# A graph attention kernel in two layers: paired statistics, the tiles of one row sum chain, and when the values are scaled

## The chip, the cores and the metric

The kernel runs on one core of one Trainium2 chip. The metric is the device time in microseconds of one execution, the median of several runs. In the profile the engines are named PE (TensorE, matmuls), PEld (its weight loads), DVE (VectorE), ACT (ScalarE), POOL (GpSimd) and SP (SyncE, which issues most of the transfers).

## The reference

Two graph attention layers follow one another on x of shape 8 x 2048 x 256 (batches, rows, channels) with one adjacency matrix of 2048 x 2048. After each layer its input is added and every row is normalised.

```python
# layer 0: 8 heads of 32 channels
x_proj = einsum('bnd,hdf->bhnf', x, W)
e = leaky_relu(e_src[..., :, None] + e_dst[..., None, :], 0.2)
e = e + softplus(beta_tilde) * log(adj + 1e-6)      # and no edge where adj is 0
h = softmax(e) @ x_proj
x1 = layernorm(x + h.reshape(B, N, D) @ W_out.T)
# layer 1: one head, dot products
e = leaky_relu((x1 @ W1) @ (x1 @ W2).T, 0.2)        # and no edge where adj is 0
out = layernorm(x1 + relu(softmax(e) @ (x1 @ W3)))
```

## The kernel before, in words

**Layer 0** (class `Gat`, one object a batch) never forms the softmax as such. The score of an edge is a function of a sum of two numbers, so its exponential is a maximum of two products. For a unit, which is one pair of heads (`hp`, 4 of them) and one tile of 128 source rows (`jt`, 16 of them), VectorE makes for each of the two heads a tile `s` of 128 x 2048 by one instruction at L375, out of the query rows `c`, a factor `re` and the adjacency tile `mt`. TensorE multiplies `s` by the scaled values `v` into `val` and, for the row sum of the softmax, by the broadcast factor `re` into `den` (both in `products`, L403 to L408). There are 4 buffers for `s`, so VectorE can be two units ahead of TensorE, and 2 buffers for `mt`, which is loaded again from memory for every unit (L202).

**The row sum chain** takes some of the den products away from TensorE. The table `SUMMED` (L68, L69) lists for each batch and pair the tiles that are chained. For the first of them ScalarE makes `d`, a copy of `s` scaled by the factor (L392). For each later one VectorE adds the scaled `s` to `d`, one unit later (L386). For these tiles there is no den product; after the last tile one product with ones adds `d` to `den` (L397). Each later chain tile costs VectorE two long instructions, and saves TensorE one den product.

**Layer 1** (class `Dot`) takes 16 steps a batch: scores, exponential, transposes and the product with h3, with row statistics at the end. Its matmuls are full size, and its work for VectorE is small.

**The order.** TensorE's order is written out by hand; the other engines' instructions are put in order by the framework, by program order and by when they are ready in its own model. The main loop (L668 on) puts the layer 0 of batch b, called `fresh`, between the steps of the layer 1 of batch b - 1 through `layer_0(n)`, which runs n units. Batch 0 has no partner; its 64 units come first and share their time with `others()` (L603), which projects all other batches. Every second unit is followed by a slot in which some rows of it are projected (L658 to L662).

The first pair of each fresh batch has a place of its own: its 16 units lie around the end of the batch before. Units 0 to 5 share it with two steps of the old layer 1. Then six groups follow, with two units in each of the first five: groups 0 to 3 make x1 (`output`, four row tiles at a time: matmul with W_out, addition of x, statistics, normalisation), groups 2 to 5 turn it (`turn`: transposes and h3). Before the first group VectorE also has to multiply the heads by the reciprocal row sums (`finish`, L448). Tile numbers in what follows are these units.

**x1's statistics** (L476 to L483): for each row tile of 256 channels one `bn_stats`, which writes count, mean and sum of squared deviations for the even and for the odd elements, and one `bn_aggr`, which joins them to mean and variance.

**The scaling of the values** (`scale`, L290 to L294) multiplies the projected values of a quarter of a batch by the factor, 128 x 1024 elements. `factors()` (L276) has to precede it, and `store()` (L296) follows for the batches whose values go to memory. `others()` holds a list `later` with the three scalings and the store that remain, and takes one entry off at every row it projects (L635).

Of the kernel before, what the change touches and what calls it, by code (L numbers as in the profile page):

```python
# [9 lines left out]
F32 = mybir.dt.float32  # L10
BF16 = mybir.dt.bfloat16
I32 = mybir.dt.int32
AF = mybir.ActivationFunctionType
ALU = mybir.AluOpType
# [4 lines left out]
P = 128  # L19
# [8 lines left out]
def kernel(  # L28
# [26 lines left out]
    nc = tc.nc  # L55
    B, N, D = x.shape
    H, _, DH = w_proj.shape
# [3 lines left out]
    NB = N // BK  # L61
    HALF = N // 2
    HP = 2
    NP = H // HP
    IG = BK // P


    SUMMED = [[()] * NP, [()] + [(1, 4, 7, 10, 13)] * (NP - 1)]  # L68
    SUMMED += [[(2, 4, 5)] + [(1, 3, 5, 7, 9, 11, 13)] * (NP - 1)] * (B - 2)  # L69

    const = ctx.enter_context(tc.tile_pool(name="const", bufs=1))
    dram = ctx.enter_context(tc.tile_pool(name="dram", bufs=1, space=DRAM))
# [3 lines left out]
    small = ctx.enter_context(tc.tile_pool(name="small", bufs=3))  # L76
# [3 lines left out]
    def mm_tile(name):  # L80
        return ps.tile([P, BK], F32, tag="mm", name=name)
# [15 lines left out]
    eps_ln = const.tile([P, 1], F32)  # L97
# [36 lines left out]
    def later_weights():  # L134

        nc.sync.dma_start(w3s, w3.rearrange("(k p) d -> p k d", p=P))
        w1t, w2t = (chunk.tile([P, KC, D], F32, tag="pt", name=name, bufs=2) for name in ("w1t", "w2t"))
        for w, dst in ((w_out, wot), (w1, w1t), (w2, w2t)):
            src = [row_tile("square") for _ in range(KC)]
            for o in range(KC):  # L140
                nc.sync.dma_start(src[o], w[ts(o, P), :])
            yield
            for kc in range(KC):
                t = mm_tile("sq_t")
                for o in range(KC):
                    nc.tensor.transpose(t[:, ts(o, P)], src[o][:, ts(kc, P)], ident)
                nc.scalar.copy(dst[:, kc, :], t[:, 0:D])
        yield
        for dc in range(KC):
            t = mm_tile("w12p")  # L150
            for kc in range(KC):
                nc.tensor.matmul(t[:, 0:D], w1t[:, kc, ts(dc, P)], w2t[:, kc, :], start=(kc == 0), stop=(kc == KC - 1))
            nc.scalar.copy(w12[:, dc, :], t[:, 0:D])
        yield
# [75 lines left out]
    def row_tile(name, bufs=4):  # L230
        return small.tile([P, D], F32, tag="row", name=name, bufs=bufs)


    class Gat:
# [216 lines left out]
        def output(self):  # L451


            b = self.b
            xb = x[b].rearrange("(t p) d -> p t d", p=P)
            xs = []

            def load(g):
                xs.append(chunk.tile([P, IG, D], F32, tag="ht", name="xg", bufs=3))
                nc.sync.dma_start(xs[g], xb[:, ts(g, IG), :])  # L460

            load(0)
            yield
            for g in range(NB):
                if g < NB - 1:
                    load(g + 1)
                st = small.tile([P, IG, nc.vector.BN_STATS_DIM], F32, name="st4", bufs=1)
                mv = small.tile([P, IG, nc.vector.BN_AGGR_DIM], F32, name="mv4", bufs=2)
                z = self.ht[:, ts(g, IG)].rearrange("p t k i -> p t (k i)")
                for k in range(0, IG, 2):  # L470
                    y = mm_tile("y").rearrange("p (t c) -> p t c", t=2)
                    for i in range(2):
                        for kc in range(KC):
                            nc.tensor.matmul(y[:, i, :], self.ht[:, g * IG + k + i, kc, :], wot[:, kc, :],  # L474
                                             start=(kc == 0), stop=(kc == KC - 1))
                    nc.vector.tensor_add(z[:, k:k + 2, :], y, xs[g][:, k:k + 2, :])  # L476
                    for i in range(k, k + 2):
                        nc.vector.bn_stats(st[:, i, :], z[:, i, :])
                        nc.vector.bn_aggr(mv[:, i, :], st[:, i, :])
                f = small.tile([P, 2, IG], F32, name="f4", bufs=2)  # L480
                nc.scalar.activation(f[:, 0, :], mv[:, :, 1], AF.Ln, bias=eps_ln)
                nc.scalar.activation(f[:, 0, :], f[:, 0, :], AF.Exp, scale=-0.5)
                nc.vector.scalar_tensor_tensor(f[:, 1, :], mv[:, :, 0], -1.0, f[:, 0, :], ALU.mult, ALU.mult)  # L483
                for k in range(IG):
                    nc.scalar.activation(z[:, k, :], z[:, k, :], AF.Identity, bias=f[:, 1, k:k + 1],
                                         scale=f[:, 0, k:k + 1])
                nc.scalar.dma_start(x1_d[b].rearrange("(t p) d -> p t d", p=P)[:, ts(g, IG), :], z)
                yield
# [114 lines left out]
    def others():  # L603


        order = gats[2:-2] + gats[1:2] + gats[-2:]
        groups = [(gat, g) for gat in order for g in range(NB)]
        xgs, xts, later = [], [], []

        def load(n):  # L610
            if n < len(groups):
                xgs.append(load_x(groups[n][0].b, groups[n][1]))

        def turn(n):
            if n < len(groups):
                xts.append(chunk.tile([P, KC, BK], F32, tag="ht", name="xt", bufs=3))
                transpose_x(xgs[n], xts[n])
                load(n + 1)

        load(0)  # L620
        yield
        turn(0)
        for n, (gat, g) in enumerate(groups):
            if g == 0:
                if gat is order[-1]:

                    for _ in range(IG):
                        later.pop(0)()
                        yield
                gat.begin("h3" if n // NB % 2 or gat is order[-1] else "v")  # L630
            for k in range(IG):
                gat.row(g * IG + k, xts[n])
                if k == 1:
                    turn(n + 1)
                if later:  # L635
                    later.pop(0)()
                if g == NB - 1 and k == IG - 1:
                    gat.factors()
                    gat.scale(0)
                    later = [lambda gat=gat, i=i: gat.scale(i) for i in range(1, NB)]  # L640
                    if gat.b > 1:
                        later.append(gat.store)
                if g == 0 and k == IG - 1 and n > 0:
                    groups[n - 1][0].queries()
                yield
        for work in later:
            work()
        order[-1].queries()
        yield

    projections, weights = others(), later_weights()
    next(projections)
    count = (B - 1) * NT + IG
    for k in range(1, NP * NT + 1):
        g0.step()
        if k == NP * NT:
            gats[1].load_ahead()
        if k % 2 == 0:  # L658
            for _ in range(k * count // (NP * NT) - (k - 2) * count // (NP * NT)):
                next(projections)  # L660
            if k > NT:
                next(weights, None)  # L662

# [4 lines left out]
    for b in range(1, B + 1):  # L668
        gat, fresh = gats[b - 1], gats[b] if b < B else None

        def layer_0(count):
            if fresh:
                fresh.step(count)

        if b > 1 and fresh:
            fresh.follow(gat)
            values = fresh.load()
            next(values)
            fresh.later.append(values)
        rows, turns = gat.output(), gat.turn()  # L680
        if dot is None:
            layer_0(4)
            next(projections)
            next(rows)
        else:

            dot.step(lambda k: layer_0((0, 2, 2)[k]))
            if not fresh:
                for work in gat.later:
                    for _ in work:  # L690
                        pass
            next(rows)
            dot.step()
        layer_0(2)

        for g in range(NB + 2):
            if g < NB:
                next(rows)
            if g > 1:
                next(turns)  # L700
                if g == NB + 1:
                    dot = Dot(gat)
                next(turns)
            if g < NB + 1:
                layer_0(2)
        dot.scores(0)
        dot.step(lambda k: layer_0((2, 0, 2)[k]))
        count = NP * NT - 20
        for i in range(NT - 3):
            n = (i + 1) * count // (NT - 3) - i * count // (NT - 3)  # L710
            dot.step(lambda k: layer_0((0, n - 2, 2)[k]))
# [31 lines left out]
```

## Time and profile before

| what | value |
|---|---|
| time, median of 3 runs | 4389.91 us (4386.79 to 4391.33) |
| span of the profiled execution | 4393.1 us |
| mean granted TensorE clock | 0.989 |
| `s`, L375 | 1024 instructions, 2342 ns each |
| chain additions, L386 | 264 instructions, 2344 ns each |
| chain copies, L392 (ScalarE) | 54 instructions, 2006 ns each |
| x1's bn_stats, L478, and bn_aggr, L479 | 128 of each, 411 and 169 ns |
| scaling, L294 | 32 instructions, 1219 ns each |
| VectorE waiting for `mt` transfers | 58.3 us in 33 waits |

The line numbers are those of the kernel before. The busy time of TensorE is a union of its instructions, and a matmul's end is modelled, so that a stretch with TensorE busy throughout needn't be one at full rate; the granted clock stands beside it for that. A line of a timeline gives start, length, engine, line, operation and tiles, how many instructions are merged in it, and in brackets the idle time before it with what ended it. In a list of waits, a line gives who waited for whom, the total, the number of waits and the longest.

### The profile page before, as it was taken

The numbers are of one execution on the slowest core, as the hardware profiler recorded it, in microseconds if no ns is written. First come the engines' busy times: TensorE is split into PE (matmuls) and PEld (weight loads), VectorE is DVE, ScalarE is ACT, GpSimd is POOL, SyncE is SP. The second block draws the span as 40 slices with busy tenths as digits, with TensorE's granted clock in tenths as the row PEclk, the third lists the DMA queues.
The fourth block names the chain that finished last, engine by engine and source line by source line (L and its number), as shares of the span: only waits on it lengthen the run. The fifth ranks groups of instructions, "written<-read, shape, count | busy, mean of one in ns | idle before, by whom it ended". The sixth has DMA issues, their size and how long they took to land.

```text
span 4393.1 us, 59809 instructions
## 1 busy us (share of the span) xinstructions
PE 4245.8 (97%) x25072; PEld 2220.1 (51%) x25072; DVE 3603.9 (82%) x2606; ACT 1661.8 (38%) x3019; POOL 9.5 (0%) x14
## 2 busy tenths in 40 slices
PE   7999899998999999999999999999999999999999
PEld 4444354544555545554555545555455545555666
DVE  6888878988799989889789988989799987998222
ACT  6522143332433333333343333333333324333455
POOL 0000000000000000000000000000000000000000
PEclk9999999999999999999999999999999999999999
DMA  8877756656455564556555464555544565543211
GB/s 251 303 256 262 264 193 221 223 191 229 174 192 190 204 213 148 194 183 217 193 180 199 159 232 171 195 187 211 194 177 167 183 224 191 184 174 143 78 48 41
DMA packets 253166, 839.10 MB, mean 191 GB/s; under 512 B 32224, under 2 KB 150752, under 8 KB 178400
## 3 DMA queue, kind: packets, MB, share of 16 engines
q1 hardware_dynamic: 217568, 801.71, 51.5%
q10 hardware_dynamic: 35328, 33.56, 2.3%
q8 instruction: 196, 3.21, 0.3%
q14 instruction: 74, 0.61, 0.0%
HBM read 761.53 MB, written 73.14 MB: 190 GB/s over the span
## 4 chain that ended last, share of the span: by engine, by line
PE 56%; DVE 20%; issue 8%; DMA 7%; ACT 2%; SPq 1%; POOL 0%; DVEq 0%; ACTq 0%; POOLq 0%
DVE s L375 14%; PE e L534 14%; PE val L406 12%; PE acc L573 12%; PE den L406 9%; PE pt L557 3%; DMA mt<-mt_d 3%; DVE d L386 3%; PE h3p L505 2%; PE h1p L524 2%; DMA rb<-rec_d 1%; DVE p L539 1%; DMA xg<-in_x_dram 1%; PE y L474 1%; PE proj L270 1%
## 5 line engine op out<-in xcount | busy, mean ns | idle before, releaser
L375 DVE SCALAR_TENSOR_TENSOR s<-c,re,mt 128x2048 f32<-128x2048 f32 x1024 | 2353.6, 2342 | 225.4 <-PE den L406 150.8
L406 PE MATMUL val<-s,v 128*32 128x512 f32 x8192 | 1041.2, 606 | 84.9 <-DVE s L375 84.9
L573 PE MATMUL acc<-h,pts 128*128 128x256 f32 x4096 | 954.4, 381 | 16.7 <-ACT pts L559 16.6
L534 PE MATMUL e<-x1t,h 128*128 128x512 f32 x2048 | 904.5, 594 | 3.3 <-ACT h L526 3.2
L573 PEld LDWEIGHTS acc<-h,pts 128*128 128x128 f32 x4096 | 747.9, 190 | 113.0 <-ACT pts L559 28.4
L406 PE MATMUL den<-s,re 128*32 128x512 f32 x5648 | 727.1, 601 | 0.0
L386 DVE SCALAR_TENSOR_TENSOR d<-s,re,d 128x2048 f32<-128x2048 f32 x264 | 615.0, 2344 | 0.0
L534 PEld LDWEIGHTS e<-x1t,h 128*128 128x128 f32 x2048 | 380.2, 190 | 450.1 <-issue 415.6
L406 PEld LDWEIGHTS val<-s,v 128*32 128x32 f32 x8192 | 245.6, 110 | 707.1 <-issue 517.1
L559 ACT COPY pts<-pt 128x512 f32<-128x512 f32 x512 | 296.3, 582 | 690.2 <-PE pt L557 689.4
L539 DVE CUSTOM_DVE_ANT_0 p<-p,pen 128x2048 f32<-128x2048 f32 x128 | 292.6, 2286 | 225.3 <-ACT p L536 225.1
L536 ACT ACTIVATE p<-e 128x512 f32<-128x512 f32 x512 | 304.4, 595 | 455.4 <-PE e L534 447.7
L406 PEld LDWEIGHTS den<-s,re 128*32 128x32 f32 x5648 | 198.0, 112 | 436.1 <-issue 429.7
L557 PEld LDWEIGHTS pt<-ident,p 128*128 128x128 f32 x2048 | 239.0, 141 | 219.8 <-issue 174.7
L542 ACT ACTIVATE p<-p,neg 128x2048 f32<-128x2048 f32 x128 | 256.7, 2005 | 208.5 <-DVE neg L539 208.5
L557 PE MATMUL pt<-ident,p 128*128 128x128 f32 x2048 | 318.1, 279 | 5.1 <-ACT p L542 5.1
L579 DVE TENSOR_TENSOR z<-z,x1r 128x256 f32<-128x256 f32 x128 | 54.0, 422 | 182.9 <-ACT z L578 181.5
L578 ACT ACTIVATE z<-acc,rec 128x256 f32<-128x256 f32 x128 | 60.6, 473 | 373.4 <-PE acc L573 286.8
L270 PE MATMUL proj<-wp,xt 128*128 128x272 f32 (+1 forms) x512 | 130.9, 401 | 2.3 <-ACT v L272 1.2
L505 PE MATMUL h3p<-w3s,x1t 128*128 128x256 f32 x512 | 122.7, 383 | 4.8 <-ACT x1t L500 4.3
L272 ACT COPY v<-proj 128x256 f32<-128x256 f32 x128 | 46.9, 376 | 206.4 <-PE proj L270 192.4
L474 PE MATMUL y<-wot,ht 128*128 128x256 f32 x512 | 118.3, 385 | 0.0
(89 smaller groups left out, 1926.8 us busy)
## 6 DMA issues: line engine op xcount, KB each, us to landing
mt<-mt_d SPq DMA_DIRECT2D x496, 1024.0 KB
c<-c_d SPq DMA_DIRECT2D x64, 1024.0 KB
pen<-pen_d SPq DMA_DIRECT2D x112, 512.0 KB
xg<-in_x_dram SPq DMA_DIRECT2D x60, 512.0 KB
adj_t<-in_adj_dram SPq DMA_DIRECT2D x16, 1024.0 KB
mt_d<-mt SPq DMA_DIRECT2D x16, 1024.0 KB
rb<-rec_d SPq DMA_DIRECT2D x128, 128.0 KB
x_d<-ht ACTq DMA_DIRECT2D x32, 512.0 KB
```

Source lines behind the costliest of these rows:

```text
L270: nc.tensor.matmul(t[:, 0:cols], xt[:, kc, ts(it % IG, P)], wp[:, kc, 0:cols], start=(kc == 0), stop=(kc == KC - 1))
L375: nc.vector.scalar_tensor_tensor(sa, self.cs[a], self.re[:, 0, jt, h:h + 1], mt, ALU.max, ALU.mult)
L386: nc.vector.scalar_tensor_tensor(d, sa, e[:, jt - 1, h:h + 1], d, ALU.mult, ALU.add)
L406: nc.tensor.matmul(dst[ts(q, DH), ts(c, BK)], weights[q % 2], s[q % 2][:, ds(q // 2 * HALF + c * BK, BK)], start=start, stop=stop)
L505: nc.tensor.matmul(t[:, ts(i, D)], x1t[:, kc, ts(2 * (j - 1) + i, P)], w3s[:, kc, :], start=(kc == 0), stop=(kc == KC - 1))
L534: nc.tensor.matmul(t, self.h1[:, kc, ts(it % IG, P)], self.x1t[:, kc, ts(c, BK)], start=(kc == 0), stop=(kc == KC - 1))
L536: nc.scalar.activation(p[:, ts(c, BK)], t, AF.Prelu, alpha=ALPHA)
L539: nc.vector.tensor_tensor_reduce(p, p, pen, -1.0, FMAX, ALU.add, ALU.min, neg)
L542: nc.scalar.activation(p, p, AF.Exp, bias=neg, scale=-1.0, accum_out=den)
L557: nc.tensor.transpose(t[:, ts(k, P)], p[:, ts(g * IG + k, P)], ident)
L559: nc.scalar.copy(pt, t)
L573: nc.tensor.matmul(acc, now[:, ts(k, P)], self.h3[:, j, :], start=(j == 0), stop=(j == NT - 1))
```

## The change

Three edits, none of which changes what is computed.

1. x1's statistics of two row tiles are taken by one `bn_stats`: the two tiles are interleaved by the access pattern, so that the even elements are those of the first tile and the odd ones those of the second. Mean and sum of squared deviations are then read straight from its six numbers, and `bn_aggr` goes; the division by 256 moves into the scale of the Ln.
2. The first pair's row sum chain (batches 2 to 7) is on tiles 9, 11 and 13 and not on 2, 4 and 5. It is to take VectorE's additions out of the units in which it has x1's first groups and the reciprocals to do.
3. The list of scalings that remain is shared (`scaling`), and one entry is taken off a slot, that is, every two units, and no longer one at every projected row. What remains after the last slot is done one by one between the first four units of batch 1. This is to keep the scalings of one batch from standing together in VectorE's queue.

```diff
-    SUMMED += [[(2, 4, 5)] + [(1, 3, 5, 7, 9, 11, 13)] * (NP - 1)] * (B - 2)
+    SUMMED += [[(9, 11, 13)] + [(1, 3, 5, 7, 9, 11, 13)] * (NP - 1)] * (B - 2)
...
-                st = small.tile([P, IG, nc.vector.BN_STATS_DIM], F32, name="st4", bufs=1)
-                mv = small.tile([P, IG, nc.vector.BN_AGGR_DIM], F32, name="mv4", bufs=2)
+                st = small.tile([P, IG // 2, nc.vector.BN_STATS_DIM], F32, name="st4", bufs=2)
+                mv = st.rearrange("p a (t c) -> p (a t) c", t=2)
...
-                    for i in range(k, k + 2):
-                        nc.vector.bn_stats(st[:, i, :], z[:, i, :])
-                        nc.vector.bn_aggr(mv[:, i, :], st[:, i, :])
+                    nc.vector.bn_stats(st[:, k // 2, :], z[:, k:k + 2, :].rearrange("p t c -> p c t"))
...
-                nc.scalar.activation(f[:, 0, :], mv[:, :, 1], AF.Ln, bias=eps_ln)
+                nc.scalar.activation(f[:, 0, :], mv[:, :, 2], AF.Ln, bias=eps_ln, scale=1.0 / D)
...
-                nc.vector.scalar_tensor_tensor(f[:, 1, :], mv[:, :, 0], -1.0, f[:, 0, :], ALU.mult, ALU.mult)
+                nc.vector.scalar_tensor_tensor(f[:, 1, :], mv[:, :, 1], -1.0, f[:, 0, :], ALU.mult, ALU.mult)
...
                     for _ in range(IG):
-                        later.pop(0)()
+                        if scaling:
+                            scaling.pop(0)()
                         yield
...
-                if later:
-                    later.pop(0)()
...
-                    later = [lambda gat=gat, i=i: gat.scale(i) for i in range(1, NB)]
+                    scaling.extend([lambda gat=gat, i=i: gat.scale(i) for i in range(1, NB)])
...
-        for work in later:
-            work()
...
             for _ in range(k * count // (NP * NT) - (k - 2) * count // (NP * NT)):
                 next(projections)
+            if scaling:
+                scaling.pop(0)()
...
-            layer_0(4)
+            for _ in range(4):
+                layer_0(1)
+                if scaling:
+                    scaling.pop(0)()
```

More of the change, by code (lines that the diff above doesn't have):

```diff
@@ L607, in others @@
         groups = [(gat, g) for gat in order for g in range(NB)]
-        xgs, xts, later = [], [], []
+        xgs, xts = [], []
         def load(n):
@@ L639, in others @@
                     gat.scale(0)
-                    later = [lambda gat=gat, i=i: gat.scale(i) for i in range(1, NB)]
+                    scaling.extend([lambda gat=gat, i=i: gat.scale(i) for i in range(1, NB)])
                     if gat.b > 1:
-                        later.append(gat.store)
+                        scaling.append(gat.store)
                 if g == 0 and k == IG - 1 and n > 0:
@@ L645, in others @@
                 yield
-        for work in later:
-            work()
         order[-1].queries()
         yield
+    scaling = []
     projections, weights = others(), later_weights()
```

## The prediction

> **What bounds the kernel now.** I read the page's busy shares first, then the waits, then stretches of the span, then the timelines of VectorE and TensorE in the worst stretch.
>
> ```profile
> PE 4245.8 (97%) x25072; PEld 2220.1 (51%) x25072; DVE 3603.9 (82%) x2606; ACT 1661.8 (38%) x3019; POOL 9.5 (0%) x14
> ```
>
> TensorE is the bound: 4393.1 us of span less 4245.8 leaves 147 us in which it does nothing. Nothing in the change takes away or adds a matmul, so all it can win lies in those 147 us and in time at a reduced clock. The waits name the cause:
>
> ```profile
> DVE s L375 <- PE den L406: 150.8, 86, 4.3
> ...
> PE val L406 <- DVE s L375: 84.9, 49, 6.3
> ```
>
> Usually VectorE runs ahead until the four `s` buffers are full and waits for TensorE (150.8 us, free). Where it has fallen behind, TensorE waits for `s`: 84.9 us in 49 waits. The stretches say where:
>
> ```profile
> 310.00:335.00 25.00, 18.34 (x105) 8.37 (x104) 20.24 (x15) 5.32 (x18) 0.37 (x1) 0.80 0.71 249
> 1010.00:1064.00 54.00, 40.07 (x225) 21.37 (x227) 45.22 (x39) 16.16 (x29) 0.00 (x0) 0.94 0.68 224
> 1550.00:1580.00 30.00, 23.11 (x127) 9.29 (x126) 26.09 (x26) 4.48 (x12) 0.00 (x0) 0.83 0.55 184
> 2059.00:2089.00 30.00, 23.40 (x141) 10.10 (x143) 27.90 (x27) 4.48 (x12) 0.00 (x0) 0.89 0.56 196
> 2567.00:2597.00 30.00, 22.49 (x135) 9.61 (x137) 27.98 (x27) 4.49 (x12) 0.00 (x0) 0.89 0.49 169
> 3076.00:3106.00 30.00, 23.12 (x126) 9.41 (x127) 25.93 (x26) 4.48 (x12) 0.00 (x0) 0.83 0.55 186
> 3585.00:3615.00 30.00, 22.90 (x139) 9.54 (x141) 27.13 (x26) 4.48 (x12) 0.00 (x0) 0.89 0.51 178
> ...
> 1595.00:1640.00 45.00, 44.94 (x313) 23.64 (x313) 33.97 (x33) 16.53 (x29) 0.00 (x0) 1.00 0.66 243
> ...
> 1640.00:1963.00 323.00, 321.43 (x1828) 165.42 (x1830) 285.88 (x184) 125.82 (x213) 0.00 (x0) 1.00 0.49 173
> ```
>
> Columns: length, busy time of PE, PEld, DVE, ACT, POOL, then the granted clock. From 1640 to 1963 us TensorE is idle for 1.6 us of 323. The idle time comes back once a batch, in the first pair of the next batch, while the batch before is projected out. I add idle time and clock deficit (1 less the clock, times the length): 6.9 + 5.1, 6.6 + 3.3, 7.5 + 3.3, 6.9 + 5.1, 7.1 + 3.3, which is 55.1 us for fresh batches 3 to 7, and 13.9 + 3.2 = 17.2 for batch 2: 72.3 us. The timelines of batch 3 show who is late:
>
> ```profile
> 1543.54 2.34 DVE L386 SCALAR_TENSOR_TENSOR d<-s,re,d 128x2048 f32<-128x2048 f32 x1
> 1545.80 4.61 DVE L375 SCALAR_TENSOR_TENSOR s<-c,re,mt 128x2048 f32<-128x2048 f32 x2
> 1550.33 2.34 DVE L386 SCALAR_TENSOR_TENSOR d<-s,re,d 128x2048 f32<-128x2048 f32 x1
> ...
> 1552.92 2.35 DVE L386 SCALAR_TENSOR_TENSOR d<-s,re,d 128x2048 f32<-128x2048 f32 x1
> ...
> 1563.96 2.32 DVE L386 SCALAR_TENSOR_TENSOR d<-s,re,d 128x2048 f32<-128x2048 f32 x1
> ```
>
> ```profile
> 1559.71 1.04 PE L406 MATMUL val<-s,v 128*32 128x512 f32 x2 [1.92 <-DVE s L375]
> 1563.35 2.78 PE L406 MATMUL val<-s,v 128*32 128x512 f32 x11 [2.60 <-DVE s L375]
> ...
> 1572.16 2.70 PE L406 MATMUL val<-s,v 128*32 128x512 f32 x11 [2.37 <-DVE s L375]
> ```
>
> The four chain additions of tiles 4 and 5 sit exactly where VectorE also does the reciprocal's multiplications and the first groups of x1, with no gap from 1537.9 to 1568.7 us, and TensorE waits at tiles 6 and 7.
>
> **What the Trainium skill says.** "TensorE: Matmul & The Clock Gate", Part 1: an idle window of about 3.4 us puts the array at half clock until it has been busy for such a window. The trace agrees: the clock column falls to 0.83 or 0.89 just in the 30 us stretches with some 7 us of idle time, and is 1.00 in the others. So a removed wait brings back more than its own length. "SBUF — State Buffer", Door 1 (its note on cachelines): accesses that go to another 16-byte line each time pay a penalty; this prices the strided statistics below. The trace has a pair that agrees: L283 and L285 both take 128 elements, and the one that walks across tiles takes 370 ns, the other 282.
>
> **The change part by part.**
>
> *Chain of the first pair, tiles 2, 4, 5 to 9, 11, 13 (batches 2 to 7).* The counts stay: three den products fewer, one closing product, two copies on ScalarE (2.0 us each), four additions on VectorE. Only their place moves. Back to back an addition costs 2.27 us (1543.54 to 1545.80), so 4 x 2.27 = 9.1 us leave VectorE before tile 7. TensorE does the den products of 2, 4 and 5 again; a product's start-to-start time is about 1.72 us (val at 1581.08, den at 1582.82 in TensorE's timeline), so it reaches tile 6 later by 3 x 1.72 = 5.2 us, with real work that it saves at 9, 11 and 13. VectorE's position against TensorE thus improves by 14.3 us, against waits of 10 to 12 us with their clock. They should go, except for what the groups of x1 themselves cause. The new place: from 1595 to 1640 us VectorE is idle for 11.0 of 45 us. TensorE loses two den products there (3.4 us), VectorE gains 9.1: it is short by 1.5 us, which its lead covers (full buffers are two tiles, 4 x 2.27 = 9 us of work). The copies fall on ScalarE when tile 9's `s` is made, at about 1584 to 1589 us; ScalarE had been idle for 18.3 us before 1589.2, so they fit if they come early. I leave 3 us of waits in each of six phases: 72.3 - 18 = 54 us won.
>
> *Scaling a group a slot (batch 0).* Before, four scalings run as a block. At 315.4 us it is followed by the longest wait of the trace:
>
> ```profile
> 315.40 4.63 DVE L294 TENSOR_TENSOR v<-v,re 128x1024 f32<-128x1024 f32 x4 [0.63 <-ACT re L288]
> ```
>
> TensorE then waits 6.31 us before its val at 323.55. Moving three to later slots takes 3 x 1.14 = 3.4 us out of that wait, and what is left should cost less clock. The stretch lost 6.7 + 5.0 = 11.7 us (0.80 of clock); I take 7. The stretches 140 to 160 us (15.01 busy, clock 0.83: 8.4 lost) and 430 to 450 us (15.83, 0.83: 7.6 lost) have the same block; there the masks, and the loop that must empty the list before the last batch, keep some of it: 4.5 and 3.5. Together 15 us. The store of v goes out about two slots later than now; what waits for it is ScalarE's copy into the same buffer two batches on (a wait of 13.5 us on this store occurs once now), and behind that copy the projection's matmuls. It lands within a slot or two and I cost it at nothing.
>
> *Scaling in the opening of batch 1.* Three scalings move by a tile or two in a stretch (490 to 515 us) where VectorE is busy 23.8 of 25 us. Work moved inside a full stretch brings little: 1 us.
>
> *Statistics.* Per pair of tiles two bn_stats (411 ns each) and two bn_aggr (169 ns each) go, 1.16 us. One bn_stats over 512 elements comes. Low bound: 411 ns plus 256 more elements at 1.08 ns, the rate that lies between a bn_stats of 256 elements and an `s` of 2048 ((2342 - 411) / 1792), 0.69 us. High bound: on top of it the strided surplus of 88 ns per 128 elements, four times, 1.04 us. I take 1.0, as every element is 1 KB from the last: 0.16 us x 64 pairs = 10 us of VectorE, most of it beside matmuls; 1 us on the path. The factors read the six numbers directly, with no more instructions than before.
>
> Sum: 54 + 15 + 1 + 1 = 71 us; 4389.9 - 71 = 4319 us.
>
> **The rivals.**
> - *The wait moves with the chain* (0.13). For: the 1.5 us shortage at tiles 12 to 15, and that `s` of tile 13 needs a buffer that the additions of tile 11 still read. Against: the free time of VectorE there. 7 us of wait and clock in six phases, 42 us: about 4360.
> - *Transfers become the bound* (0.10). `mt` has two buffers; with VectorE on time, TensorE asks for 1 MB every 5.3 us (two tiles and a y group, 10.6 us), plus about 1 MB of x and x1 per group: some 300 GB/s, where 370 GB/s (530 to 550 us) is the most that I found in a stretch of 20 us. 5 us in six phases, 30 us: about 4349.
> - *All waits go* (0.20), those at tiles 8 and 9 and in batch 1 too: 18 + 11 us more, about 4290.
> - *Slower* (0.07). The two copies delay the normalisation and the x1 transposes behind them on ScalarE by 4 us (24 us in six phases), the additions stall tiles 12 and 14 by 7 us with 3.4 us of clock (62 us): 86 against 71, about 4405.
>
> **How the numbers follow.** The forecast of 4319 has 0.50. The range of 4285 to 4365 takes in the first three rivals and leaves out the slower one and the tails. Faster by over 0.2% (under 4381) gets 0.88, since four of the cases lie there but each can be smaller than drawn; within, 0.05; slower, 0.07.
>
> **What would show it.** Right: TensorE's waits for `s` fall from 84.9 to some 25 us; the clock is 1.00 in all six phases at tiles 6 and 7; VectorE's free time at tiles 10 to 15 shrinks; the block of four L294 is broken up; the new bn_stats takes 0.7 to 1.05 us. Wrong: a new wait for `s` or `x1t` at tiles 12 to 15, more waits on `mt` transfers, or on the store of v. If waits at tiles 6 and 7 stay with the additions gone, the multiplications and groups of x1 were the cause and not the chain.

## The result, and the profile after

| kernel | time, median | ratio to before (95% interval) |
|---|---|---|
| before | 4389.8 us | 1 |
| after | 4348.4 us | 0.9907 (0.989 to 0.9924) |
| after, a second time, on the chip of the last experiments | 4347.7 us (before there 4393.9) | 0.9902 (0.9887 to 0.9916) |

The change saves 41 us where 71 were forecast; the time lies in the range. The profiled span fell from 4393.1 to 4346.3 us and the mean granted clock rose from 0.989 to 0.995. The stretches after, placed on the same tiles as those shown of before (length, busy time of PE, PEld, DVE, ACT, POOL, clock):

```profile
1005.00:1059.00 54.00, 48.77 (x306) 25.80 (x308) 41.41 (x30) 9.23 (x23) 0.00 (x0) 0.94 0.68 234
1540.00:1570.00 30.00, 29.46 (x203) 13.63 (x196) 27.74 (x21) 9.80 (x16) 0.00 (x0) 1.00 0.57 202
2042.00:2072.00 30.00, 29.46 (x204) 13.70 (x197) 27.83 (x21) 9.70 (x16) 0.00 (x0) 1.00 0.57 201
2544.00:2574.00 30.00, 29.46 (x204) 13.72 (x197) 27.92 (x21) 9.65 (x15) 0.00 (x0) 1.00 0.58 202
3046.00:3076.00 30.00, 29.46 (x201) 13.72 (x194) 28.05 (x21) 9.51 (x15) 0.00 (x0) 1.00 0.58 200
3548.00:3578.00 30.00, 29.47 (x201) 13.74 (x194) 28.06 (x21) 9.51 (x15) 0.00 (x0) 1.00 0.57 201
...
1576.00:1612.00 36.00, 33.65 (x240) 16.75 (x232) 35.28 (x20) 8.45 (x17) 0.00 (x0) 1.00 0.62 222
```

In the five stretches of batches 3 to 7 TensorE is now idle for 0.5 us each and never at a reduced clock: 2.7 us in place of 55.1. In batch 2 it is 5.2 us idle and 3.2 us of clock, in place of 17.2. So in batches 3 to 7 the waits that the chain was moved for are gone, and in batch 2 about half of them. The last line, tiles 10 to 15 of batch 3, is new: VectorE is busy for 35.28 of 36 us, and TensorE idle for 2.35 us. TensorE's timeline in batch 3 shows both:

```profile
1548.18 1.92 PE L406 MATMUL val<-s,v 128*32 128x512 f32 x16
1549.92 1.90 PE L406 MATMUL den<-s,re 128*32 128x512 f32 x16
...
1552.82 1.49 PE L406 MATMUL val<-s,v 128*32 128x512 f32 x11 [0.16 <-DVE s L375]
...
1560.03 1.92 PE L406 MATMUL val<-s,v 128*32 128x512 f32 x16
...
1599.40 2.02 PE L406 MATMUL val<-s,v 128*32 128x512 f32 x13
...
1604.46 1.04 PE L406 MATMUL val<-s,v 128*32 128x512 f32 x2 [0.89 <-DVE s L375]
1606.72 1.49 PE L406 MATMUL val<-s,v 128*32 128x512 f32 x11 [1.22 <-DVE s L375]
...
1609.34 0.59 PE L406 MATMUL den<-d,ones 128*32 128x512 f32 x1
```

Tile 6 starts at 1548.18 and tile 8 at 1560.03 us: 11.9 us with a group of x1 between, where it was 1559.71 to 1581.08, 21.4 us, before. But tiles 14 and 15, from 1599.40 to the closing product at 1609.34, take 9.9 us, where four products of 1.72 us would take 6.9. In all, from the first tile of batch 2 to the last of batch 7, the kernel gains 39 us: 35 in the first pairs of batches 3 to 7 and 4 in that of batch 2.

What did not come is the gain in batch 0. VectorE's timeline of after, where the block of four scalings stood before, and TensorE's behind it:

```profile
314.41 3.50 DVE L294 TENSOR_TENSOR v<-v,re 128x1024 f32<-128x1024 f32 x3 [0.62 <-ACT re L288]
317.83 1.22 DVE L448 TENSOR_TENSOR ht<-ht,rb 128x1024 f32<-128x1024 f32 x1
318.96 1.22 DVE L294 TENSOR_TENSOR v<-v,re 128x1024 f32<-128x1024 f32 x1
```

```profile
322.49 1.91 PE L406 MATMUL val<-s,v 128*32 128x512 f32 x2 [6.24 <-DVE s L375]
```

Three scalings still stand together, the fourth one instruction later, and the wait of 6.31 us is one of 6.24. The wait at 436 us is as long as before, 4.18 us. From 140 to 160 us TensorE does better (4.8 us of idle time and clock in place of 8.4), but by the starts of its tiles 3 us are lost again between 189 and 203 us. TensorE's waits for `s` in total:

```profile
PE val L406 <- DVE s L375: 48.1, 41, 6.2
```

They were 84.9 us; I expected some 25.

### The profile page after: what moved, and what is told of

Same layout as the page of the kernel before. It is cut to its first block, busy times and chain, and to the rows that moved or that the text cites. A ratio compares the mean times of both kernels' runs of the same rounds, so it can differ in the third digit from the quotient of the medians.

```text
span 4346.3 us, 59625 instructions
## 1 busy us (share of the span) xinstructions
PE 4235.9 (97%) x25072; PEld 2224.6 (51%) x25072; DVE 3588.2 (83%) x2414; ACT 1663.6 (38%) x3019; POOL 9.5 (0%) x14
## 4 chain that ended last, share of the span: by engine, by line
PE 55%; DVE 18%; issue 8%; DMA 4%; ACT 2%; SPq 0%; DVEq 0%; ACTq 0%
PE e L533 15%; PE acc L572 14%; DVE s L375 12%; PE val L406 11%; PE den L406 8%; PE pt L556 4%; DVE d L386 3%; PE h1p L523 2%; DMA mt<-mt_d 2%; DVE p L538 1%; PE h3p L504 1%; DMA rb<-rec_d 1%; ACT p L541 1%; PE y L475 1%; DMA adj_r<-in_adj_dram 1%
## 5 line engine op out<-in xcount | busy, mean ns | idle before, releaser
L406 PE MATMUL val<-s,v 128*32 128x512 f32 x8192 | 1030.6, 600 | 48.1 <-DVE s L375 48.1
L406 PE MATMUL den<-s,re 128*32 128x512 f32 x5648 | 710.4, 593 | 0.0
L392 ACT ACTIVATE d<-s,re 128x2048 f32<-128x2048 f32 x54 | 107.6, 2007 | 51.0 <-DVE s L375 51.0
```

What stands on the lines that cost most here:

```text
L406: nc.tensor.matmul(dst[ts(q, DH), ts(c, BK)], weights[q % 2], s[q % 2][:, ds(q // 2 * HALF + c * BK, BK)], start=start, stop=stop)
```

## The experiments

Twelve kernels ran, the kernel after a second time among them. Each is compared with the kernel before on its own chip, so the ratios are what to compare.

**The three parts alone.** The chain alone (`e1_chain`):

```diff
-    SUMMED += [[(2, 4, 5)] + [(1, 3, 5, 7, 9, 11, 13)] * (NP - 1)] * (B - 2)
+    SUMMED += [[(9, 11, 13)] + [(1, 3, 5, 7, 9, 11, 13)] * (NP - 1)] * (B - 2)
```

> The kernel before with the first pair's chain on tiles 9, 11, 13 and nothing else. Theory A (the chain's additions in the wrong place made TensorE wait at tiles 6 and 7): the six phases give nearly what they give in the whole change, where the batches 2 to 7 came out 39 us shorter; 33 to 40 us less than before, about 4352. Theory B (VectorE's shorter queue by the paired statistics did it, 25.7 us less busy): at most 15 us less, 4375 or more.

Measured: 0.9942 (0.9928 to 0.9955), by the ratio 25.5 us less than the 4395.5 us of before on that chip. That is neither theory's number, but the larger part. The waits at tiles 6 and 7 are gone but for 0.45 us (tile 6 to 8 takes 9.2 us less than before in batch 3), and the new wait at tile 15 is longer than in after:

```profile
1618.94 1.05 PE L406 MATMUL val<-s,v 128*32 128x512 f32 x2 [1.34 <-DVE s L375]
1621.21 2.78 PE L406 MATMUL val<-s,v 128*32 128x512 f32 x11 [1.22 <-DVE s L375]
```

The second line's 11 matmuls take 2.78 us and not 1.49: here the wait also costs the clock.

The statistics alone (`e2_stats`) are the change's hunk in `output()` and nothing else.

> The kernel before with the paired statistics and nothing else. Theory A: VectorE is 25.7 us less busy (69.0 to 43.3), mostly beside matmuls, but the groups of x1 in batch 1 gain: 4 to 10 us less, about 4383. Theory B: 25 us or more less, under 4365.

Measured: 0.998 (0.9972 to 0.9987), 9 us less; most of it in the first pairs of batches 1 and 3 to 7, from tile 6 to 10.

The scaling alone (`e3_scaling`) has the `scaling` list and leaves the chain and the statistics as they were.

> The kernel before with the scaling's list taken off a group a slot and nothing else. Theory A (VectorE's order still has three of four scalings together, so the waits at about 317 and 436 us stay): 0 to 5 us less, about 4387, and both waits still 6 and 4 us long. Theory C (the spreading works and is worth what the prediction gave it): 15 us less, 4375.

Measured: 0.9992 (0.9984 to 1.0), 3.5 us less or nothing. The program asks for one scaling a slot, but the order of VectorE's instructions follows it only in part. In the kernel before, five of the seven blocks have no `s` between their four scalings. In the trace of `e3_scaling` three still have none, three have four `s` in front of the last scaling alone, and one has `s` in two places. Why the framework puts them so is not shown.

By the ratios the three alone give 25.5 + 9 + 3.5 = 38 us, and together 41. The whole without the scaling's edit (`e8_no_scaling`: the first two diffs on the kernel before), and after once more beside it (`r_after`):

> The kernel before with the chain on 9, 11, 13 and the paired statistics, without the scaling's edit: what that edit is worth in the whole change. If the parts add up (0.9942, 0.998 and 0.9992 each alone), the ratio is 0.992, 3 us more than after; if the scaling's edit does nothing or harm, 0.991 or less.

> The kernel after once more, beside the run without the scaling's edit on the same chip: 0.9907 as measured first, within 0.0015.

Measured: 0.9919 (0.9904 to 0.9934) and 0.9902 (0.9887 to 0.9916). The scaling's edit is worth 8 us here by the medians (4356.0 and 4347.7), with intervals that overlap. By the starts of the tiles in the two traces, 4 us of the difference come at tiles 6 to 12 of batch 1 and some 3 in the first pair of batch 0, and none at the block shown above.

**What makes the new wait at tile 15.** Fewer additions on the same tiles (`e6_chain_9_11`), none at all (`e7_chain_none`), and additions where VectorE had idle time (`e4_chain_123`), each on the kernel after:

```diff
-    SUMMED += [[(9, 11, 13)] + [(1, 3, 5, 7, 9, 11, 13)] * (NP - 1)] * (B - 2)
+    SUMMED += [[(9, 11)] + [(1, 3, 5, 7, 9, 11, 13)] * (NP - 1)] * (B - 2)      # e6
+    SUMMED += [[()] + [(1, 3, 5, 7, 9, 11, 13)] * (NP - 1)] * (B - 2)           # e7
+    SUMMED += [[(1, 2, 3)] + [(1, 3, 5, 7, 9, 11, 13)] * (NP - 1)] * (B - 2)    # e4
```

> The kernel after with the first pair's chain on tiles 9 and 11 alone: two additions fewer on VectorE (4.5 us), one den product more on TensorE (1.7 us) a phase. Theory A (the wait at tile 15 is VectorE's lead used up by the additions): the 3.9 us there go, 2.2 us less in each of six phases, 13 us less than after: ratio to before about 0.988. Theory E (the wait at tile 15 comes from the mt transfers or the order): it stays, 10 us more than after, 0.993.

> The kernel after with no chain in the first pair: no addition at all, two den products more than after (3.4 us a phase). Theory A: no wait at tiles 6, 7 or 15, so 3.9 - 3.4 = 0.5 us less in each of six phases, 3 us less than after, ratio about 0.990: the place of the chain would then have brought no more than having none. Theory E: 0.995.

> The kernel after with the first pair's chain on tiles 1, 2, 3, so that its additions fall on tiles 3 and 4, where VectorE was idle for 8.7 us in the kernel after (1518 to 1541 us). Theory A (the new wait at tile 15 comes from the additions of tiles 11 and 13 that use up VectorE's lead): the wait at tile 15 goes and none comes at tiles 6 and 7, 3.9 us in each of six phases, about 4325. Theory D (the lead is needed at tile 6 whatever comes before it): waits at tiles 6 and 7 come back, 4350 or more.

Measured: e6 0.9876 (0.9861 to 0.9891), 4339.4 us; e7 0.9885 (0.9872 to 0.9899); e4 0.9945 (0.9933 to 0.9958). The first two answer as theory A: VectorE's additions make the wait. The transfers of theory E are no part of it, as in after VectorE is never idle from the start of tile 10 until the `s` of tile 15 are made. TensorE's timeline of e6, tiles 14 and 15 of batch 3, has no wait left:

```profile
1602.30 1.93 PE L406 MATMUL val<-s,v 128*32 128x512 f32 x16
1604.04 1.90 PE L406 MATMUL den<-s,re 128*32 128x512 f32 x16
1605.76 1.90 PE L406 MATMUL val<-s,v 128*32 128x512 f32 x16
1607.47 1.90 PE L406 MATMUL den<-s,re 128*32 128x512 f32 x16
1609.19 1.90 PE L406 MATMUL den<-d,ones 128*32 128x512 f32 x16
```

6.9 us from 1602.30 to the closing product, the 3 us less that the four products should take. Kernel e7 tells what the place had to give, in tiles 6 to 9 and in tiles 10 to 15 of batch 3:

```profile
1541.00:1577.00 36.00, 35.22 (x239) 18.15 (x232) 34.44 (x26) 7.42 (x17) 0.00 (x0) 1.00 0.61 209
...
1577.00:1613.00 36.00, 35.94 (x269) 18.54 (x262) 25.52 (x16) 11.98 (x24) 0.00 (x0) 1.00 0.65 239
```

Without additions VectorE has 36 - 25.5 = 10.5 us free in tiles 10 to 15 and 1.6 us in tiles 6 to 9. But what is free after the `s` of tile 15 are made can't help tile 15. These are the instructions that make the `s` of tiles 14 and 15, and TensorE's val of tile 15, in the kernel before:

```profile
1617.60 9.14 DVE L375 SCALAR_TENSOR_TENSOR s<-c,re,mt 128x2048 f32<-128x2048 f32 x4 [2.37 <-PE den L406]
```

```profile
1628.85 1.90 PE L406 MATMUL val<-s,v 128*32 128x512 f32 x16
```

and in e7:

```profile
1595.81 9.14 DVE L375 SCALAR_TENSOR_TENSOR s<-c,re,mt 128x2048 f32<-128x2048 f32 x4 [3.71 <-PE den L406]
```

```profile
1607.06 1.90 PE L406 MATMUL val<-s,v 128*32 128x512 f32 x16
```

In both, VectorE had waited for a free buffer and was done 2.1 us before TensorE's val. From the start of tile 10 to that point it is idle for 6.2 us in the kernel before, for 7.1 in e7 and for nothing in after. VectorE's lead, from the end of a tile's second `s` to the start of its val, in us, in batch 3:

| tile | 10 | 11 | 12 | 13 | 14 | 15 |
|---|---|---|---|---|---|---|
| before | 7.2 | 3.8 | 7.0 | 3.2 | 3.2 | 2.1 |
| e7, no additions | 7.3 | 3.9 | 7.0 | 3.5 | 3.2 | 2.1 |
| after | 5.6 | 2.1 | 2.8 | -0.1 | -0.5 | -2.2 |

The lead is the same with the waits at tiles 6 and 7 and without them. The additions use it up.

With the chain on 1, 2, 3 (e4) theory D holds: the wait at tile 15 is gone, and waits come at tiles 5 and 7.

```profile
1537.84 1.04 PE L406 MATMUL val<-s,v 128*32 128x512 f32 x2 [1.24 <-DVE s L375]
1540.17 1.49 PE L406 MATMUL val<-s,v 128*32 128x512 f32 x11 [1.28 <-DVE s L375]
...
1551.71 1.04 PE L406 MATMUL val<-s,v 128*32 128x512 f32 x2 [0.69 <-DVE s L375]
1554.05 1.49 PE L406 MATMUL val<-s,v 128*32 128x512 f32 x11 [1.29 <-DVE s L375]
```

The 8.6 us in which VectorE had been idle there were no spare time. A chain there takes three den products from TensorE (5.2 us) and gives VectorE 9.1 us, a swing of 14.3 us.

**What holds `s` up at 317 us.** Leave out what stands before it (`e10_left_out`, on the kernel before):

```diff
-                    later = [lambda gat=gat, i=i: gat.scale(i) for i in range(1, NB)]
+                    later = []
```

> The kernel before, with three of the four scalings of each batch 1 to 7 left out (21 instructions of 1.2 us; the first quarter's stays): its output is not the reference's. It bounds what spreading the scalings can bring. If the block is the cause of the waits at about 317 and 436 us, they fall to about 3 and 1 us and the kernel takes 15 to 25 us less (0.9955); if the wait before the block (for the factors through ScalarE and GpSimd) is the cause, they stay over 4 us and it takes under 8 us less (0.998 or more).

Measured: 0.9973 (0.9963 to 0.9984), 11 us less. The two waits answer differently. The one at 436 us falls from 4.17 to 0.77 us, so there the block is the cause. The one at 317 us grows to 12.33 us; it begins at 312.8 us, where it was 317.2, and ends 1.6 us later than before. VectorE's timeline of e10 there:

```profile
308.85 0.37 DVE L280 TENSOR_REDUCE top<-both 128x8 f32<-128x128 f32 x1 [4.06 <-ACT both L274]
...
310.98 1.23 DVE L294 TENSOR_TENSOR v<-v,re 128x1024 f32<-128x1024 f32 x1 [0.64 <-ACT re L288]
320.34 1.23 DVE L448 TENSOR_TENSOR ht<-ht,rb 128x1024 f32<-128x1024 f32 x1 [8.13 <-DMA rb<-rec_d]
322.75 9.14 DVE L375 SCALAR_TENSOR_TENSOR s<-c,re,mt 128x2048 f32<-128x2048 f32 x4 [1.18 <-DMA mt<-mt_d]
```

VectorE stands still for 8.13 us, in front of `s`, at the multiplication that waits for the transfer of the reciprocals, and then for 1.18 us more, for the `mt` tile of that `s`. Before, the scalings had filled that time. Two more kernels leave the multiplication and its transfers out in batch 0, with the scalings left out too (`e12_no_rb`, on e10) and with all of them in (`e13_no_rb_alone`, on the kernel before):

```diff
-            if lo == 0:
+            if lo == 0 or b == 0:
                 return
```

> As the kernel with three scalings of four left out, and batch 0 also leaves out the multiplication of its heads by the reciprocal row sums and the eight transfers of rb for each half of the heads; its output is not the reference's. With the scalings left out, the wait at about 313 us had grown to 12.3 us, with VectorE's queue standing 8.1 us at that multiplication for its transfer. If that is the cause, the wait falls under 3 us; if the factors or the mt transfer are, it stays over 5 us.

> The kernel before, with all its scalings, and batch 0 leaves out the multiplication by the reciprocal row sums and its rb transfers; its output is not the reference's. If the scalings are what holds s up at about 317 us, the wait there stays at 5 us or more (1.1 us less for the multiplication); if they only fill the time in which the rb transfer is under way, it falls under 3 us.

Measured: 0.9923 (0.9906 to 0.9939) and 0.9968 (0.9956 to 0.9979). In both the wait at 317 us is gone. VectorE's timeline of e13, with the block of four whole:

```profile
306.68 4.61 DVE L375 SCALAR_TENSOR_TENSOR s<-c,re,mt 128x2048 f32<-128x2048 f32 x2
311.20 0.35 DVE L280 TENSOR_REDUCE top<-both 128x8 f32<-128x128 f32 x1
...
313.32 4.63 DVE L294 TENSOR_TENSOR v<-v,re 128x1024 f32<-128x1024 f32 x4 [0.64 <-ACT re L288]
317.87 6.87 DVE L375 SCALAR_TENSOR_TENSOR s<-c,re,mt 128x2048 f32<-128x2048 f32 x3
```

One pair of `s` more is made before the factors, and that lead covers the block: TensorE does two tiles from 310.19 us on without a wait. But these two kernels don't tell the multiplication from the transfers. SyncE's queue, in the kernel before:

```profile
311.39 0.96 SPq L442 DMA_DIRECT2D rb<-rec_d  x2
312.45 0.37 SPq L202 DMA_DIRECT2D mt<-mt_d  x1
```

and in e13:

```profile
290.24 11.44 SPq L202 DMA_DIRECT2D mt<-mt_d  x4
```

In the kernel before, the `mt` tile that the late `s` needs is asked for at 312.45 us, behind the last of the reciprocals and a load of x that waits for TensorE until 310.93, and by the semaphores in the trace it lands at 321.05 us; the `s` starts at 321.14. With neither scalings nor multiplication ahead of it, it could still not have started sooner. In after the tile lands at 319.07 and the `s` starts at 320.10 us, so the scalings cost 1 us there. In e10 it lands at 322.65 us, after the multiplication. In e13, without the reciprocals' transfers, it is asked for by 301.7 us. So what holds `s` up at this wait is, but for 1 us, a late `mt` transfer. How much of its lateness comes from its place in SyncE's queue, and how much from the buffers that the reciprocals share with every second `mt` tile (L201, L437), is open. Both kernels leave work out that the kernel needs; how to have the transfers earlier was not tried.

**Scalings on another engine** (`e11_pool`, on e6):

```diff
-            nc.vector.tensor_tensor(v, v, e.unsqueeze(2).to_broadcast([P, IG * H, DH]), ALU.mult)
+            nc.gpsimd.tensor_tensor(v, v, e.unsqueeze(2).to_broadcast([P, IG * H, DH]), ALU.mult)
```

> The kernel after with the chain on tiles 9 and 11 and all scalings on GpSimd, which is idle at those times. If VectorE's queue alone counts, the waits at 317 and 436 us shrink to 3 us or less and it takes 10 to 20 us less than the chain on 9 and 11 alone; if GpSimd's access holds VectorE up, nothing is gained or it is slower.

Measured: 0.9942 (0.993 to 0.9955), 30 us slower than the same chain with the scalings on VectorE. GpSimd takes 3947 ns for one (median; the shortest 1903) where VectorE takes 1219. In the trace the waits for `s` fall little (36.3 to 34.7 us in total), and others come: 13.3 us at 459 us for a projection whose copy on ScalarE is held up. The wait at 317 us, now at 310, is still 6.12 us long, with no scaling in VectorE's queue; there VectorE waits for `mt`:

```profile
308.01 4.62 DVE L375 SCALAR_TENSOR_TENSOR s<-c,re,mt 128x2048 f32<-128x2048 f32 x2 [4.18 <-DMA mt<-mt_d]
```

GpSimd also slows VectorE down. An `s` beside a scaling takes up to 4005 ns; the longest in e6, where GpSimd does no scaling, is 2365. These are the shortest, the median and the longest `s` of e11:

```profile
L375 DVE SCALAR_TENSOR_TENSOR s<-c,re,mt x1024: 2251/2347/4005, 37.5 to 4024.2; 128x2048 f32<-128x2048 f32 x171
```

## Why the prediction was right in direction and too large

*Bound and mechanism.* Shown. TensorE waited because of the chain on tiles 2, 4 and 5: the edit alone takes the waits at tiles 6 and 7 away but for 0.45 us (e1), and with no chain at all they are away as well (e7). The runs move VectorE's additions and TensorE's den products together, so they don't say which of the two weighs more. Their clock came back with them, as the Trainium skill ("TensorE: Matmul & The Clock Gate", Part 1) lets one expect: 0.83 to 0.89 became 1.00. The page's idle window of about 3.4 us is not the measure of a single gap, though: those at tile 6 of batch 3 are 1.92 and 2.60 us, two matmuls apart, and in e1 1.34 and 1.22 us were enough. And the clock was below 1.00 not only in the 30 us stretches, but also in those at 310 and 1010 us, which have idle time too.

*The 3 us left in each phase.* This step failed: "it is short by 1.5 us, which its lead covers". Both sizes in it were wrong. Of the 11.0 free microseconds that I had read between 1595 and 1640 us, 4.9 come after the `s` of tile 15 are made; 6.2 can be used, or 7.1 with the paired statistics. And the lead at tile 15 is 2.1 us, not the 9 us that full buffers take to make. With these sizes the sum is 9.1 + 3.4 - 7.1 = 5.4 us, of which 2.1 are covered; some 3 us are missing, and tiles 14 and 15 take 3 us too long. Without the paired statistics it is more (e1), and then it also costs the clock. The rival in which the wait moves with the chain gave 7 us a phase. From the start of tile 10 to that of the next pair e1 takes 53.0 us where before takes 50.0, with two den products (3.4 us) fewer: 6.4 us a phase. In the whole change it is 50.7 us, some 4 us a phase. So for the chain alone, worth some 25 us and not 54, that rival was nearly right. In batch 2, where the sum had 17.2 - 3 = 14 us, 4 came. That the rival of the transfers had 4349 is chance: VectorE's waits for `mt` are 59.0 us in after and were 58.3.

*The scalings, 15 us.* Wrong in two ways. The list spreads the calls in the program, but VectorE's order hardly follows it (e3), so the blocks at 317 and 436 us stay. And even with three of four left out the kernel gains only 11 us (e10), as the longest wait isn't theirs: the `s` there needs an `mt` tile that lands at 321.05 us, 0.09 us before the `s` starts. I had named the block ahead of the late `s` as its cause. That the store of v costs nothing held: its one wait is still a single one, of 13.6 us.

*The opening of batch 1* was given 1 us. Batch 0 and 1 together gained 10 us in the profiled pair, 7 us of it in batch 1 and 6 of these at its tiles 6 to 12, where the statistics (2 us in e2) and the scaling's edit (4 us, e8 against r_after) meet.

*The statistics, 1 us,* were undersized. The group after is

```profile
L478 DVE BATCH_NORM_STATS2 st<-ht 128x6 f32<-128x512 f32 x64 | 43.3, 697 | 0.3
```

697 ns is close to my low bound (0.69 us) and not the 1.0 us taken. And VectorE's time wasn't beside other work: in the groups of x1 it is the late engine, so 26 us less of it (69.0 to 43.3) gave 9 on the path (e2).

*The fastest version* is the chain on tiles 9 and 11 with the other two edits, 4339.4 us at 0.9876; after has 0.9907 and 0.9902, with intervals that touch or overlap. By the starts of the tiles from batch 2 on it gains 45 us on before, where after gains 39 and 40. Having no chain in that pair (0.9885) does about as well, so chaining the third tile there cost more than it brought. What is left in the first pair of batch 2 (5.2 us idle and 3.2 us of clock) was not tried.

## What to carry to other kernels

Before moving work into an engine's free time, count that time only up to the moment at which its result is needed, and take the lead as it stands there: of 11.0 us, 6.2 could be used here, and the lead was 2.1 us where a full set of buffers is 9 us of work. Moving work from engine A to engine B over the same stretch counts twice, once as the work that B gains and once as the time that A no longer takes. And before an instruction is blamed for the one that follows it in a queue, look up when each input of the late one arrived, and leave the suspect out: if the queue then stands still for something else, it was only filling the time. A kernel that leaves out an instruction and its transfers moves the other transfers too.

## What the runs showed of the hardware

- A `bn_stats` over two interleaved tiles, each element 1 KB from the one before, costs no surcharge: 697 ns for 512 elements, against an estimate of 687 from 411 ns and 256 more elements at 1.08 ns. The Trainium skill ("SBUF — State Buffer", Door 1) lets one expect a penalty for a new 16-byte line at each access, and L283 against L285 (370 and 282 ns) had looked like it; for this instruction the measurement decides, and says there is none.
- Equal waits need not cost the same. In the last batch TensorE waits 2.40 us for the first h3 in the kernel before, and 2.29 us in after, in both of its traces. These are TensorE's lines, of before, of after and of after a second time:

```profile
4096.23 1.99 PE L505 MATMUL h3p<-w3s,x1t 128*128 128x256 f32 x8 [2.40 <-ACT x1t L500]
```

```profile
4046.40 3.53 PE L504 MATMUL h3p<-w3s,x1t 128*128 128x256 f32 x8 [2.29 <-ACT x1t L499]
```

```profile
4044.62 1.99 PE L504 MATMUL h3p<-w3s,x1t 128*128 128x256 f32 x8 [2.29 <-ACT x1t L499]
```

The same eight matmuls take 1.99, 3.53 and 1.99 us: the clock was 1.00 from 4095 to 4099 us in the first, 0.57 from 4046 to 4050 us in the second, and 1.00 again from 4044 to 4048 us in the third, which is the same kernel. The Trainium skill ("TensorE: Matmul & The Clock Gate", Part 1) says that the window in which idleness is judged runs free of the program, and this agrees with it. From the first tile of the last pair to the end after takes 344.5 us in its first trace, where before takes 341.6; in its second it takes 341.9, so that this loss is not the change's.
- GpSimd can hold VectorE up. In e11 an `s` that runs beside a scaling on GpSimd takes up to 4005 ns, where the median is 2347.
